# Two edits at the seam between attention and feed-forward: one load moved to GpSimd's queue, and an attention scope whose pools are laid in another order

## The chip, the cores and the metric

The kernel runs on one core of one Trainium2 chip. The metric is device microseconds (us) of one launch, less is better. A launch is timed several times and the median is given; one further execution was recorded by the hardware profiler, and the views below are read from its trace. Engines are named as the profile names them: PE (TensorE matmul), PEld (its weight loads), DVE (VectorE), ACT (ScalarE), POOL (GpSimd), SP (SyncE, which does nothing here but issue DMAs). SPq, ACTq and POOLq mark what an engine's queue does beside computing, DMA issues above all.

## The reference, cut to what matters

Four images of 64 x 64 pixels and 256 channels, in f32, pass through two layers:

```python
# layer 0: group norm, deformable convolution (8 groups x 9 bilinear samples), residual
x = x + conv(_gn(x), ...)
# layer 1, on 4096 tokens an image: additive attention, then a feed-forward part for half the tokens
t = t + attn(_ln_t(t), Wt, Wx, bh, Wa, ba)
t = t + ffn(_ln_t(t), wr, br, w1, b1, w2, b2)

def attn(inputs, ...):
    q = inputs @ Wt;  k = inputs @ Wx.T                  # 32 units each
    beta = tanh(q[:, :, None, :] + k[:, None, :, :] + bh)  # 4096 x 4096 x 32
    a = softmax(beta @ Wa[:, 0] + ba)
    return a @ inputs

def ffn(x, ...):
    weights = x @ wr + br                                # one number per token
    sel = the 2047 tokens with the largest weights
    y = (gelu(x[sel] @ w1 + b1) @ w2 + b2) * weights[sel]
    return x + (y at sel, 0 elsewhere)
```

## The kernel before, in words

**Stages.** After a stage that works out offsets and weights for all images and the sampling of image 0, a loop runs over the images n = 0 to 3. Each turn has two parts. In the first, three generators are advanced in a hand-written order of turns: `feed_forward(n - 1)`, `attention_prep(n)` and `sample_image(n + 1)`. In the second, `attention(n)` runs, with what is left of the sampling in its gaps. After the loop `feed_forward(3)` runs alone: the tail.

**Sampling** loads weights (`wb`, L692, two buffers) and rows (`xs`, L687) on SyncE, multiplies and adds them on DVE (L701, L709), and stores tokens from SyncE. Some "exact rows" are gathered again by an indirect DMA of GpSimd (L585, L590, into `xre`) and combined on DVE (L663, into `tte`).

**attention_prep(n)** loads the tokens, normalises and transposes them, and works out exponentials: `kf` for the keys stays in SBUF, those for the queries (`qe`, L838) are stored to DRAM (`qf_d`, by ScalarE's queue).

**attention(n)** takes 512 queries at a time. `queries(q)` loads their factors from `qf_d` into `qf` (L881, on SyncE) and makes `qn` of them (L884, two operations of GpSimd). Then, for each tile of 128 keys and each of three pairs of terms: `d` products on PE (L898), Ln into a tile `r` on ACT (L992), Exp (L994), `nn` products on PE (L908) and a quotient on DVE (L913); sums on POOL and DVE (L998, L1000, L1002, L1005), an Exp on ACT (L920), and the product with the values on PE (L936), whose result DVE adds up (L960). L859 is PE's last work of attention_prep.

**feed_forward(n)** chooses the tokens and scatters all rows by 32 indirect DMAs of GpSimd (L1304) into `sort_d`, the chosen ones first. Then it works on four chunks of 512 rows. `chunk(s)` loads the rows (L1336, its output named `big` in the profile) and waits for all 32 scatters before that. It normalises them on ACT (L1344), transposes them (`transpose4`, L784 and L785) into `xT`, and adds on POOL (L1350) and DVE (L1352). For each chunk, 8 products `ph` on PE with a gelu on ACT (L1364, L1365) and 4 products `py` on PE (L1370) follow; DVE combines (L1373), and an indirect DMA of GpSimd scatters the rows into the output (L1377). `chunk(s + 1)` is called within chunk s, after its second `py`.

**What sets the order.** The framework's planner fixes, when the kernel is built, the order of instructions in each engine's queue; each queue then runs in that order. DVE operations marked as pinned keep the order of the program; they are all recorded by one helper, line L259.

**Pools.** Tiles live in pools of SBUF. A scope lists its pools as (name, buffers, memory); those of SBUF are laid one after another in the listed order from the scope's base. A pool that lies over a pool of the scope before waits until that one is done. The scope of the first part, which stays as it is, is

```python
("one", 1, 0), ("two", 2, 0), ("sb", 2, 0), ("row", 2, 0), ("rp", 3, 0),
```

`one` holds `big`; w1 and w2 lie above it in `one`; `two` holds small statistics and `si`, `sb` small tiles, `row` the `xT`, `rp` the tiles `qe` and transposed tokens. In the attention scope `rp` holds the tiles `r` (six), `qp` holds `qf` and `qn`, `ep` the weights `et`, `ap` the sums of L960, `sb` small tiles, `tte` and `xre` among them. The tail's scope has the same names without `rp`.

Of the kernel before, what the change touches and what calls it, by code (L numbers as in the profile page):

```python
# [36 lines left out]
PVB = 8  # L37
# [8 lines left out]
def layers_kernel(ctx: ExitStack, tc: tile.TileContext, a, out: bass.AP):  # L46
    nc = tc.nc
# [192 lines left out]
    @contextmanager  # L240
    def scope(*pools):

        with ExitStack() as st:
            for name, bufs, psum in pools:
                kw = {"space": PSUM} if psum else {}
                setattr(S, name, st.enter_context(tc.tile_pool(name=name, bufs=bufs, **kw)))
            yield
            for name, _, _ in pools:
                delattr(S, name)
# [494 lines left out]
    def sample_any(n):  # L744

        num = nc.values_load(large[0:1, n : n + 1], min_val=0, max_val=L)
        with tc.If(num > P), scope(
            ("smp", 2, 0), ("two", 2, 0), ("sb", 2, 0), ("dn", 1, 0), ("ps_t", 1, 1), ("ps_m", 1, 1)
        ):
            cur = S.two.tile([P, 1], F32, tag="cur", name="cur")  # L750
            nc.vector.tensor_copy(cur, part)
            with tc.For_i(0, NT, 1):
                exact = []
                for _ in exact_rows(n, cur, exact):
                    pass
                put_rows(n, *exact[0])
                nc.vector.tensor_scalar(cur, cur, float(P), None, ALU.add)
# [21 lines left out]
    def transpose4(dst, src, vec=nc.vector):  # L779

        pt = S.ps_d.tile([P, CC, 512], F32, tag="d", name="ptt")
        for k in range(CC):
            for t in range(4):
                nc.tensor.transpose(pt[:, k, t * P : (t + 1) * P], src[:, t, k * P : (k + 1) * P], ident)  # L784
        vec.tensor_copy(dst, pt)  # L785
# [462 lines left out]
    def feed_forward(n, vec):  # L1248
# [81 lines left out]
        def chunk(s):  # L1330

            o = nh + s % 2 * nx
            xs = big[:, o : o + nx].rearrange("p (t c) -> p t c", t=4)
            o = nh + 2 * nx + s % 2 * nv
            vs = big[:, o : o + nv].rearrange("p (t c) -> p t c", t=4)
            get = nc.sync.dma_start(  # L1336
                out=xs, in_=sort_d[n][s * 512 : (s + 1) * 512].rearrange("(t p) c -> p t c", p=P)
            )
            for ins in put:
                tc.add_manual_dep(get.ins, ins.name, in_order, reason="rows in order")  # L1340
            si = S.two.tile([P, 4], I32, tag="si", name="si")
            vec.tensor_scalar(si, xs[:, :, C + 3], float(n * L), None, ALU.add)
            for t in range(4):
                nc.scalar.activation(  # L1344
                    vs[:, t, :], xs[:, t, :C], AF.Identity, bias=xs[:, t, C + 1 : C + 2], scale=xs[:, t, C : C + 1]
                )
            xT = S.row.tile([P, CC, 512], F32, tag="vT", name="xT")
            transpose4(xT, vs, vec)

            nc.gpsimd.tensor_tensor(vs, vs, xs[:, :, :C], ALU.add)  # L1350
            for t in range(4):
                vec.scalar_tensor_tensor(  # L1352
                    vs[:, t, :], b2, xs[:, t, C + 2 : C + 3], vs[:, t, :], ALU.mult, ALU.add
                )
            held[s] = xs, vs, si, xT

        chunk(0)
        yield
        for s in range(NSORT // 512):
            xs, vs, si, xT = held.pop(s)  # L1360
            for f in range(FF // P):
                ph = S.ps_m.tile([P, 512], F32, tag="pm", name="ph")
                for k in range(CC):
                    nc.tensor.matmul(ph, w1[:, k, rows(f)], xT[:, k, :], start=(k == 0), stop=(k == CC - 1))  # L1364
                S.tables.append(nc.scalar.activation(hT[:, f, :], ph, AF.Gelu_apprx_tanh, bias=b1[:, f, :]))  # L1365
            yield
            for t in range(4):
                py = S.ps_m.tile([P, C], F32, tag="pm", name="py")
                for f in range(FF // P):
                    nc.tensor.matmul(  # L1370
                        py, hT[:, f, rows(t)], w2[:, f, :], start=(f == 0), stop=(f == FF // P - 1)
                    )
                vec.scalar_tensor_tensor(  # L1373
                    vs[:, t, :], py, xs[:, t, C + 2 : C + 3], vs[:, t, :], ALU.mult, ALU.add
                )
                m = min(P, NSEL - s * 512 - t * P)
                nc.gpsimd.indirect_dma_start(  # L1377
                    out=out_rows, out_offset=bass.IndirectOffsetOnAxis(ap=si[:m, t : t + 1], axis=0),
                    in_=vs[:m, t, :], in_offset=None,
                )  # L1380
                if t == 1 and s + 1 < NSORT // 512:
                    chunk(s + 1)
                yield
# [23 lines left out]
    for n in range(NB):  # L1407
        with scope(("att", 1, 0), ("smp", 2, 0), ("dn", 1, 0)):
            v = S.att.tile([P, NT, C + 1], F32, name="v")
            kf = S.att.tile([P, 2, L], F32, name="kf")  # L1410

            sampling = sample_image(n + 1) if n + 1 < NB else iter(())
            S.gather = False
            with scope(
                ("one", 1, 0), ("two", 2, 0), ("sb", 2, 0), ("row", 2, 0), ("rp", 3, 0),
                ("ps_d", 2, 1), ("ps_n", 1, 1), ("ps_m", 3, 1),
            ):


                main = feed_forward(n - 1, pinned) if n else iter(())  # L1420
                prep = attention_prep(n, v, kf, pinned)
                if n:
                    turns = (
                        "mos" + "m" * 3 + "mo" * 8 + "om" + "oss" * 2 + "m" + "oss" * 7 + "m" + "oss" * 3
                        + ("m" + "ossss" * 3 + "msss" * 4) * 4
                    )
                else:
                    turns = "o" * 10 + "s" + "os" * 24
                for turn in turns:
                    next({"m": main, "o": prep, "s": sampling}[turn], None)  # L1430
                for rest in (main, prep):
                    for _ in rest:
                        pass
            S.gather = True
            with scope(
                ("two", 2, 0), ("sb", 2, 0), ("rp", 6, 0), ("qp", 2, 0),
                ("ep", 2 * PVB + 1, 0), ("ap", 1, 0), ("ps_d", 2, 1), ("ps_n", 3, 1), ("ps_m", 1, 1),
            ):
                attention(n, v, kf, [sampling])
        attention_any(n)  # L1440
        if n + 1 < NB:
            sample_any(n + 1)
# [39 lines left out]
```

## Time and profile before

| | |
|---|---|
| time, median of 3 runs | 10574.97 us (10574.79 to 10576.85) |
| the profiled execution, whole | 10547.94 us |
| its span in the profile | 10546.2 us |
| mean granted clock of TensorE | 0.916 |
| busy share of the span | PE 86%, PEld 42%, DVE 81%, ACT 70%, POOL 50% |
| moved by DMA | 766.00 MB, mean 73 GB/s |

The profiled execution is 27.0 us (0.26%) below the median of the timed runs.

How to read the lines shown below. The timeline of an engine has one line per group of like instructions that follow each other: start and duration in us, engine, line of the kernel, operation, output<-inputs by the program's names, shapes where they are given, how many (x3), and in brackets the time that the engine stood idle before it and what ended that idleness. "[4.41 <-DMA out_dram<-big,si]" is 4.41 us of idleness ended by the landing of a DMA from `big` (addressed by `si`) to the output. A line on SPq or POOLq is the issue of a DMA; its landing is later. The view of waits has: waiting line, releaser, then us in total, number of waits and the longest. Releasers are inferred from semaphore events.

### The profile page before, as it was taken

Reading aid. Unit: us, or ns where it says so; the run is one execution under the profiler, and the core shown is the slowest. Engines: PE = TensorE matmul, PEld = TensorE weight load, DVE = VectorE, ACT = ScalarE, POOL = GpSimd, SP = SyncE. Lnnn points to the kernel's source line nnn. Section 1 sums busy time; section 2 is a strip of 40 time slices with the busy share of each in tenths; the row PEclk is TensorE's granted clock in tenths of the full one; section 3 lists DMA queues with packets and bytes.
Section 4 is the critical chain, followed back from the end, with each engine's and each line's share of the span. In section 5 each row is a group of like instructions: output and inputs, shape, how many; then the busy total and the mean of one; then the engine's idle time right before and its main releaser. Section 6 shows DMA issues by size and latency. Waiting matters only on the chain. (4 is left out here: it accounts for less than half of the span.)

```text
span 10546.2 us, 115935 instructions
## 1 busy us (share of the span) xinstructions
PE 9022.3 (86%) x38460; PEld 4384.6 (42%) x38460; DVE 8536.6 (81%) x13342; ACT 7374.7 (70%) x8389; POOL 5276.0 (50%) x3059
## 2 busy tenths in 40 slices
PE   7881039999999788999999689999999699999995
PEld 4541014444444343444444344444444344444443
DVE  7776879898989778989899679899898367777772
ACT  4450018888888537888888438888888379999991
POOL 0004207676555326767655327677555155555552
PEclk8995569999999888999999789999999799999997
DMA  3336642222212252212111342122111300000002
GB/s 120 108 137 184 206 164 70 61 67 61 70 64 74 95 168 63 52 54 58 53 55 51 115 154 53 53 53 55 52 57 43 101 13 9 10 8 7 7 5 75
DMA packets 381329, 766.00 MB, mean 73 GB/s; under 512 B 49104, under 2 KB 212592, under 8 KB 380688
## 3 DMA queue, kind: packets, MB, share of 16 engines
q1 hardware_dynamic: 324432, 678.78, 19.7%
q0 software_dynamic: 30144, 45.87, 2.8%
q10 hardware_dynamic: 26112, 33.56, 0.9%
q8 instruction: 309, 5.06, 0.2%
q14 instruction: 332, 2.72, 0.1%
HBM read 580.88 MB, written 177.14 MB: 72 GB/s over the span
## 5 line engine op out<-in xcount | busy, mean ns | idle before, releaser
L913 DVE TENSOR_TENSOR r<-nn,r 128x512 f32<-128x512 f32 x6144 | 3937.1, 681 | 862.2 <-PE nn L908 805.6
L908 PE MATMUL nn<-qn,kf 32*128 32x512 f32 (+1 forms) x12288 | 4518.9, 640 | 131.9 <-DVE r L913 95.7
L998 POOL TENSOR_TENSOR r<-r 128x1024 f32<-128x1024 f32 x1024 | 2709.6, 2646 | 2635.7 <-DVE r L913 2623.6
L992 ACT ACTIVATE r<-d 128x1024 f32<-128x1024 f32 x3072 | 3114.0, 1014 | 1089.0 <-DVE r L1002 693.3
L898 PE MATMUL d<-qf,kf 32*128 32x512 f32 (+1 forms) x12288 | 3341.3, 632 | 77.2 <-DMA qf<-qf 43.0
L994 ACT ACTIVATE r<-r 128x1024 f32<-128x1024 f32 x3072 | 3124.1, 1051 | 32.7
L908 PEld LDWEIGHTS nn<-qn,kf 32*128 32x128 f32 (+1 forms) x12288 | 1399.4, 185 | 1896.4 <-DVE r L913 1443.2
L936 PE MATMUL pv<-v,et 128*128 128x257 f32 x8192 | 2107.1, 401 | 15.0 <-DVE acv L960 15.0
L936 PEld LDWEIGHTS pv<-v,et 128*128 128x128 f32 x8192 | 1509.9, 194 | 980.5 <-issue 772.8
L898 PEld LDWEIGHTS d<-qf,kf 32*128 32x128 f32 (+1 forms) x12288 | 1018.1, 186 | 1340.3 <-issue 725.1
L1000 POOL TENSOR_TENSOR r<-r 128x512 f32<-128x512 f32 x1024 | 1332.7, 1301 | 95.8 <-DVE r L913 20.6
L701 DVE TENSOR_TENSOR prd<-xs,wb 128x1024 f32<-128x1024 f32 x768 | 974.5, 1269 | 51.2 <-DMA wb<-wt 48.2
L709 DVE TENSOR_TENSOR ac<-ac,prd 128x1024 f32<-128x1024 f32 x768 | 996.2, 1297 | 8.8
L630 POOL DMA_INDIRECT ga<-tab,tii x576 | 727.1, 1262 | 208.2 <-issue 116.3
L920 ACT ACTIVATE et<-et,nshift 128x512 f32<-128x512 f32 x1024 | 723.9, 707 | 28.2 <-DVE et L1005 28.2
L1002 DVE TENSOR_TENSOR r<-r 128x512 f32<-128x512 f32 x1024 | 720.9, 704 | 4.1 <-POOL r L998 3.7
L1005 DVE TENSOR_TENSOR et<-r 128x512 f32<-128x512 f32 x1024 | 695.7, 679 | 0.4
L115 ACT ACT_TABLE_LOAD x9 | 11.5, 1283 | 797.9 <-DVE mv L259 700.0
L725 PE MATMUL pmo<-outwp,ac 128*128 128x256 f32 x512 | 136.1, 416 | 469.6 <-DVE ac L709 431.9
L480 POOL MEMSET w<- 128x1600 f32 x16 | 22.9, 1432 | 674.3 <-DVE red L456 386.4
L725 PEld LDWEIGHTS pmo<-outwp,ac 128*128 128x128 f32 x512 | 100.9, 205 | 522.1 <-DVE ac L709 305.1
L420 PE MATMUL pc<-xn,diag 128*128 128x512 f32 x576 | 262.6, 610 | 33.4 <-ACT xn L366 33.4
(344 smaller groups left out, 5278.9 us busy)
## 6 DMA issues: line engine op xcount, KB each, us to landing
wb<-wt SPq DMA_DIRECT2D x800, 512.0 KB
tab<-tb SPq DMA_DIRECT2D x128, 256.0 KB
v<-t SPq DMA_DIRECT2D x64, 512.0 KB
xs<-xp SPq DMA_DIRECT2D x32, 680.0 KB
xp<-xp SPq DMA_DIRECT2D x32, 544.0 KB
xt<-in_x_dram SPq DMA_DIRECT2D x32, 512.0 KB
xr<-in_x_dram SPq DMA_DIRECT2D x64, 256.0 KB
t<-xr SPq DMA_DIRECT2D x64, 256.0 KB
```

What stands on the lines that cost most here:

```text
L630: keep(nc.gpsimd.indirect_dma_start(out=ga[:, s, dy].rearrange("p c e -> p (c e)"), out_offset=None, in_=tab_d[n], in_offset=bass.Indirect ...
L701: keep(nc.vector.tensor_tensor(pr.rearrange("p (r w) -> p r w", w=W), src, wb.rearrange("p (r w) -> p r w", w=W), ALU.mult,))
L709: keep(nc.vector.tensor_add(ac[:, f, :], ac[:, f, :], pr))
L898: keep(nc.tensor.matmul(d[:, j, :], kf[g, blk, rows(kt)], qs[q][0][g, blk, :], start=True, stop=True))
L908: keep(nc.tensor.matmul(nn, kf[g, blk, rows(kt)], qs[q][1][g, blk, :], start=True, stop=True))
L913: keep(nc.vector.tensor_tensor(r[:, j, :], ns[j], r[:, j, :], ALU.mult))
L920: keep(nc.scalar.activation(ets[b], ets[b], AF.Exp, bias=nshift))
L936: keep(nc.tensor.matmul(pv, ets[b0 + i][:, rows(j)], v[:, k0 + i, :], start=(i == 0), stop=(i == PVB - 1)))
L992: keep(nc.scalar.activation(rs[b, p], ds.pop((b, p)), AF.Ln))
L994: keep(nc.scalar.activation(rs[b, p], rs[b, p], AF.Exp, scale=-1.0))
L998: keep(nc.gpsimd.tensor_tensor(rs[b, 1], rs[b, 1], rs[b, 2], ALU.add))
L1000: keep(nc.gpsimd.tensor_tensor(rs[b, 1][:, 0], rs[b, 1][:, 0], rs[b, 3][:, 0], ALU.add))
```

## The change

The load of the first chunk's sorted rows (`chunk(0)`, four times in the program: one per feed-forward part) is issued by GpSimd's queue; those of chunks 1 to 3 stay on SyncE's. In the attention scope the six pools of SBUF are listed in another order: `rp` and `qp` change places with `ep` and `ap`, so that `ep` follows `sb`, then `rp`, `ap` and `qp`. Buffers, sizes and the PSUM pools stay.

```diff
@@ chunk(s), in feed_forward @@
-            get = nc.sync.dma_start(
+            get = (nc.sync if s else nc.gpsimd).dma_start(
                 out=xs, in_=sort_d[n][s * 512 : (s + 1) * 512].rearrange("(t p) c -> p t c", p=P)
             )
             for ins in put:
@@ the scope around attention(n) @@
             with scope(
-                ("two", 2, 0), ("sb", 2, 0), ("rp", 6, 0), ("qp", 2, 0),
-                ("ep", 2 * PVB + 1, 0), ("ap", 1, 0), ("ps_d", 2, 1), ("ps_n", 3, 1), ("ps_m", 1, 1),
+                ("two", 2, 0), ("sb", 2, 0), ("ep", 2 * PVB + 1, 0), ("rp", 6, 0), ("ap", 1, 0), ("qp", 2, 0),
+                ("ps_d", 2, 1), ("ps_n", 3, 1), ("ps_m", 1, 1),
             ):
```

## The prediction, made before the changed kernel was run

> **What bounds the kernel now.** I read the page first: PE, DVE and ACT are busy 86%, 81% and 70% of the span, and the chain that ended last reaches back only through the tail, so it judges neither edit. Both edits sit in the stretches between one image's attention and the next, and in the tail. There I read SyncE's own waits, then the timelines engine by engine.
>
> SyncE's waits (waiting line, releaser, us in total, times, longest):
>
> ```profile
> SPq L881 <- DMA out_dram<-big,si: 33.9, 5, 11.6
> SPq L1336 <- DMA sort<-v,rif: 27.0, 2, 25.8
> ```
>
> L881, the load of the query factors, waits for the last scatters of the feed-forward; L1336, the load of sorted rows, for the scatters into `sort`. In the stretch before image 1's attention, SyncE's queue at the second wait (start, us, what), and the engines it holds up:
>
> ```profile
> 3713.26 6.79 SPq L692 DMA_DIRECT2D wb<-wt  x3
> 3750.05 0.71 SPq L1336 DMA_DIRECT2D big<-sort  x1
> 3750.78 0.00 SPq L692 DMA_DIRECT2D wb<-wt  x1
> 3750.82 0.39 SPq L1336 DMA_DIRECT2D big<-sort  x1
> ```
> ```profile
> 3755.30 1.22 DVE L701 TENSOR_TENSOR prd<-xs,wb 128x1024 f32<-128x1024 f32 x1 [19.33 <-DMA wb<-wt]
> ```
> ```profile
> 3752.36 2.07 ACT L1344 ACTIVATE big<-big 128x256 f32<-128x256 f32 x4 [18.78 <-DMA big<-sort]
> ```
>
> No `wb` load leaves for 30 us, and DVE starves for 19.33 us of them (16.52 us before image 2's attention; image 3 has no sampling beside it). Two sorted-row loads leave together: the first is `chunk(0)`, the second `chunk(1)`, 0.77 us behind it. Next, the end of the same stretch on POOL, SP, PE, ACT and DVE:
>
> ```profile
> 3964.43 2.55 POOL L1377 DMA_INDIRECT out_dram<-big,si  x1 [4.41 <-DMA out_dram<-big,si]
> 3975.50 0.99 POOL L590 DMA_INDIRECT xre<-in_x_dram,rii  x1 [8.52 <-DMA out_dram<-big,si]
> 3978.79 3.11 POOL L884 TENSOR_SCALAR qn<-qf,csel 128x512 f32<-128x512 f32 x2 [2.29 <-DMA qf<-qf]
> ```
> ```profile
> 3974.80 0.55 SPq L881 DMA_DIRECT2D qf<-qf  x1
> ```
> ```profile
> 3978.83 2.09 PE L898 MATMUL d<-qf,kf 32*128 32x512 f32 x8 [13.64 <-DMA qf<-qf]
> ```
> ```profile
> 3981.07 1.94 ACT L992 ACTIVATE r<-d 128x1024 f32<-128x1024 f32 x2 [53.99 <-PE d L898]
> ```
> ```profile
> 3982.64 0.42 DVE L663 TENSOR_TENSOR tte<-xre,outb 128x256 f32<-128x256 f32 x1 [16.90 <-DMA xre<-in_x_dram,rii]
> 3986.39 1.29 DVE L913 TENSOR_TENSOR r<-nn,r 128x512 f32<-128x512 f32 x2 [1.96 <-PE nn L908]
> ```
>
> The last scatter lands at T = 3974.8; then follow one after another the load of `qf` (4.0 us), the first `d` products (2.2), Ln (3981.07) and the first quotient (3986.39). DVE has done nothing since 3966.
>
> **Query factors.** Who waits for whom here follows from the order of the pools. Added up from the tile sizes, the feed-forward scope lies in bytes per partition from its base at: `one` 0 to 54,240 (`big` is its first 33,280), `two` to 56,864, `sb` to 73,312, `row` to 81,504, `rp` to 93,792. Attention before: `sb` 0 to 12,416, `rp` to 36,992, `qp` to 53,376, `ep` to 88,192. After: `sb` to 12,416, `ep` to 47,232, `rp` to 71,808, `ap` to 75,936, `qp` to 92,320. Before, `qf` lies over w1 and w2, whose last reader (L1364, L1370) is a matmul; still it waits for the scatters out of `big`. So waits go by whole pools. After, `qp` lies over `row` and `rp` alone: it is free when the last `ph` has read xT and the last `qe` is stored (issued 3916.3; gelu's last wait on `ph` ends at 3925). `qf` then loads at about 3930 by my estimate (3974.80 before), and the `d` products stand behind L859, which ends near 3965, at the latest.
>
> But `rp` itself still reaches into `one` (47,232 is below 54,240). The first Ln writes an `r` tile, so it now waits for T. The stall moves from L881 to L992, and what goes is the load plus two matmuls:
> - Image 1: Ln 3981.07 to about 3974.85, 6.2 us. Image 2: 6274.14 against T = 6267.96, 6.2. Image 3: 8494.82 against 8488.57, 6.2.
>
> What is late next? The first quotient comes 5.3 us after Ln in images 1 and 3 (4.9 in image 2), so 6.2 us is the gain in image 3, where no sampling stands on DVE. In images 1 and 2 DVE's queue holds `tte`, two 0.14 us copies and an L709 of 1.20 us ahead of that quotient, 1.9 us in all, and `tte` waits for `xre`, a gather that can't leave before T (`sb` lies over `one`). It left at T + 0.7 and took 7.1 us beside two `qf` loads of 512 KB. Before image 0's attention, without those, it took 5.0 us (1592.11 to 1597.10). I take 5.0: `tte` at T + 5.7, quotient at T + 7.6. That is 3982.4 for 3986.39, a gain of 4.0, and 6275.6 for 6279.09, a gain of 3.5. With 7.1 us it would be 1.9 and 1.4.
>
> `qn` (L884, 2 x 1.56 us) moves too: from T, where DVE stands idle, to POOL's queue around 3930, between scatters, where DVE samples without pause until 3966 and so sets T. POOL has gaps there (11.1 us before 3948.09). What it does to DVE is seen in two rows: beside L1350 an L701 took 3.05 us instead of 1.22; beside `qn` in attention (4095.65) an L701 took 1.43. Bounds per image 0 to 3.1 us; I take 1.5 for images 1 and 2, 0 for image 3. The Trainium skill, "SBUF — State Buffer", section "SBUF: two separate sides", speaks against this move: a DVE instruction with two SBUF inputs and a GpSimd one that reads SBUF lock each other out for the whole instruction. By that rule alone both halves would be paid in full, 3.1 us an image; the 1.43 us row says less.
>
> Image 0's load already left early (1536.5) and its pools lie free: nothing. Sum: 4.0 + 3.5 + 6.2 - 3.0 = 10.7 us gained.
>
> **First rows by GpSimd.** Removed: one 0.71 us issue per image on SyncE, and the wait ahead of it. But the wait is not gone: `chunk(1)` stays on SyncE, depends on the same 32 scatters, needs nothing else, and stood one `wb` load behind. It takes the place. At best that one `wb` slips ahead: an L701, a `mm` and an L709, 3.1 us of DVE work, in images 1 and 2. I take 0. Moved past: on POOL the load stands behind the 32nd scatter, which it waits for; behind it is L1350, which needs the load's own rows, so nobody else waits.
>
> Cost: no row shows a plain load on POOL. The nearest is the scatter of 128 rows, 0.96 us; for 512 rows 0.96 to 3.84 us against 0.71 on SyncE, so 0.25 to 3.1 us later; or it gains up to 0.7, as the two loads no longer issue one behind the other. I take 0.5, since in the tail both chunks' transposes (x16 until 10418.4) run before the first `ph` and the second load's landing (10414.98) rules. In images 1 and 2, ACT waits 18.78 us at L1344 with a `qe` behind it, so the delay passes on. Four times 0.5 is 2.0 us; ends -2.8 and +12.4. "DMA: Bandwidth & Descriptors", section "Latency and other measured facts", gives about 1 us to the first byte from GpSimd and 0.6 from SyncE; by it four loads would lose an estimated 1.6 us. No run here shows it.
>
> Total: 10.7 - 2.0 = 8.7 us less. The profiled execution took 10547.94 us (span 10546.2 plus 1.7) and would take 10539.2; the median of the runs is 27.0 us higher and I carry the difference over: 10575 - 9 = 10566.
>
> **Rivals.**
> - Forecast, 10566 (0.48): stalls move to L992 and to `chunk(1)`. Bad end: with 7.1 us for `xre` the gains are 1.9 + 1.4 + 6.2 = 9.5; both `qn` paid in full take 2 x 3.1 = 6.2, the dearest loads 12.4: 10575 - 9.5 + 6.2 + 12.4 = 10584. Good end: gains 13.7, a `wb` slip of 2 x 3.1, `qn` free, loads -2.8: 10575 - 13.7 - 6.2 - 2.8 = 10552.
> - The whole gain is eaten, 10575 (0.07): the terms of the bad end, in part.
> - SyncE is really freed, 10535 (0.17): `chunk(1)` is queued behind more `wb` loads, and `qe` goes ahead of L1344 on ACT. Then up to 19.3 + 16.5 = 36 us of DVE idleness go; I count 31 of them, since a first `wb` still has to land, on top of the forecast's 9: 10575 - 40. Against: `chunk(1)` left 0.77 us behind `chunk(0)`.
> - `r` doesn't wait for T, 10540 (0.10): Ln starts when `py` is done, near 3966, 9 us sooner in three images, 27 in all. Against: whole-pool waits at L881, and 47,232 < 54,240.
> - Slower, 10602 (0.18): the early `qf` load is queued on SyncE ahead of `wb` loads and waits there for the last `ph` as L1336 does now. It decides once the wait outlasts the two `wb` buffers, some 5 us of L701 and L709; at the present stalls' size it costs 19.3 + 16.5 = 36 us; less the gain of 10.7 and with 2.0 for the loads that is 27 more, 10602. For it: this queue already holds two such waits. Against: `ph` is done before DVE's last ten L701 (from 3925 on).
>
> **How the numbers follow.** About 0.2%, 21 us, is what a measurement of this kernel can tell from no change. Faster by more: 0.17 + 0.10 = 0.27; slower by more: 0.18; within: 0.48 + 0.07 = 0.55. The forecast's own range is 10552 to 10584; to leave no more than 2 in 10 out it reaches down to 10540 and up to the slower rival's 10602, which leaves out only the freed queue (0.17).
>
> **What would show it.** Right: L881 issues near 3930 with no wait on `out_dram`; L992's idle time ends on that scatter, 0.1 us after T; `d` long done; L701 still starves 13 to 19 us before `chunk(1)` leaves SyncE; the `sort` load on POOL takes 1 to 4 us. Wrong: a `wb` load between 3720 and 3750; Ln before the last scatter lands; SyncE waiting at L881 with `wb` behind it.

## The result, and the profile after

The changed kernel took 10577.8 us, median of 12 runs, and the kernel before 10575.74 us beside it: a ratio of 1.0004, interval 0.9995 to 1.0013. In a second comparison (the last experiment below) the ratio was 1.0011, from 1.0001 to 1.0020. Together that is some 0.07%, 8 us, slower and no change by the bound of the prediction; the forecast gain of 9 us lies outside both intervals. The profiled execution's span was 10568.6 us. Spans of single executions differ by more than what is looked for here, since stages that the change doesn't touch vary by several us, so the traces are compared by distances within a seam (the stretch between one image's feed-forward part and the next attention).

First, the sorted rows ahead of image 1's attention. The views are the timelines of SP, POOL, DVE and ACT of the changed kernel, with the columns as before.

```profile
3741.17 0.37 SPq L1336 DMA_DIRECT2D big<-sort  x1
```
```profile
3738.51 0.96 POOL L1304 DMA_INDIRECT sort<-v,rif  x1 [0.30 <-DMA sort<-v,rif]
3741.68 0.81 POOL L1336 DMA_DIRECT2D big<-sort  x1 [2.20 <-DMA sort<-v,rif]
```
```profile
3746.60 1.23 DVE L701 TENSOR_TENSOR prd<-xs,wb 128x1024 f32<-128x1024 f32 x1 [28.22 <-DMA wb<-wt]
```
```profile
3744.84 0.60 ACT L1344 ACTIVATE big<-big 128x256 f32<-128x256 f32 x1 [32.15 <-DMA big<-sort]
3749.14 1.58 ACT L1344 ACTIVATE big<-big 128x256 f32<-128x256 f32 x3 [3.71 <-DMA big<-sort]
3750.64 1.00 ACT L839 ACTIVATE qe<-pf 128x1024 f32<-128x1024 f32 x1
```

One row on SyncE is `chunk(1)`, and it stands where `chunk(0)` stood: DVE still starves for `wb` until it has left, 28.22 us here and 25.6 in image 2. That is no growth: the second trace of the kernel before (the null run below) has 24.7 and 27.1 us there, and in the first one part of the same idleness stood at other waits. The load on POOL lands later than the one on SyncE, although it was issued only 0.51 us behind it: in this trace 7.4 us after its issue, at 3749.1. The planner has put one operation of chunk 1 ahead of chunk 0's: ACT normalises a row group of chunk 1 at 3744.84, then waits 3.71 us more for chunk 0, and the `qe` behind it starts 12.1 us after the last scatter into `sort` (3738.51). Before it was 8.4 us (3745.96 to 3754.34).

Then the seam into image 1's attention, on SP, POOL, ACT and DVE.

```profile
3915.32 1.20 SPq L881 DMA_DIRECT2D qf<-qf  x2
...
3965.08 0.81 SPq L964 DMA_DIRECT2D tr<-t  x2
```
```profile
3954.38 2.92 POOL L1377 DMA_INDIRECT out_dram<-big,si  x1 [2.65 <-DVE big L259]
3957.35 3.39 POOL L884 TENSOR_SCALAR qn<-qf,csel 128x512 f32<-128x512 f32 x2
3965.84 1.07 POOL L590 DMA_INDIRECT xre<-in_x_dram,rii  x1 [5.10 <-DMA out_dram<-big,si]
```
```profile
3972.63 1.94 ACT L992 ACTIVATE r<-d 128x1024 f32<-128x1024 f32 x2 [55.48 <-DMA xr<-in_x_dram]
```
```profile
3971.74 0.43 DVE L663 TENSOR_TENSOR tte<-xre,outb 128x256 f32<-128x256 f32 x1 [12.73 <-DMA xre<-in_x_dram,rii]
3972.08 0.14 DVE L259 TENSOR_TENSOR lo<-lo 1x1 f32<-1x1 f32 x1
3972.25 0.14 DVE L259 CAST wide<-lo 1x1 int32<-1x1 f32 x1
...
3977.64 1.89 DVE L913 TENSOR_TENSOR r<-nn,r 128x512 f32<-128x512 f32 x3 [4.11 <-PE nn L908]
```

The query factors are loaded 50 us ahead of T, as the edit says. T, the landing of the last scatter, is about 3965.05 here: L964 leaves then, having waited for it. But Ln does not start at T; it starts 7.6 us later. The bracket names a load of `xr`, which no part of Ln reads; what ends 0.24 us ahead of Ln is the copy into `wide` (3972.25 + 0.14), the last reader of `lo`, a tile of the old pool `two` over which the new `rp` lies. In image 2 it is the same 0.24 us. `wide` stands on DVE behind `tte`, which waits for `xre`, which waits for T. The first quotient comes 23.3 us after the issue of the last scatter; before it was 22.0. In image 2 it is 22.9 for 21.9.

In image 3, which has no `tte`, the seam looks as forecast at its end, but not ahead of it: POOL, SP and ACT of the changed kernel.

```profile
8490.94 0.96 POOL L1377 DMA_INDIRECT out_dram<-big,si  x1 [17.46 <-DVE big L259]
8494.10 0.96 POOL L1377 DMA_INDIRECT out_dram<-big,si  x1 [2.20 <-DVE big L259]
8499.67 0.96 POOL L1377 DMA_INDIRECT out_dram<-big,si  x1 [4.61 <-DMA out_dram<-big,si]
8503.01 2.55 POOL L1377 DMA_INDIRECT out_dram<-big,si  x1 [2.37 <-DMA out_dram<-big,si]
```
```profile
8492.32 1.21 SPq L881 DMA_DIRECT2D qf<-qf  x2
```
```profile
8514.18 1.94 ACT L992 ACTIVATE r<-d 128x1024 f32<-128x1024 f32 x2 [24.27 <-DMA out_dram<-big,si]
```

Ln waits for the last scatter alone, and the first quotient comes 16.5 us after its issue instead of 23.0. But the third scatter now waits 4.61 us, for an earlier one's landing, 7 us after 1 MB of query factors was asked for. In the kernel before:

```profile
8467.26 0.96 POOL L1377 DMA_INDIRECT out_dram<-big,si  x1 [17.50 <-DVE big L259]
8470.43 0.96 POOL L1377 DMA_INDIRECT out_dram<-big,si  x1 [2.21 <-DVE big L259]
8473.67 0.96 POOL L1377 DMA_INDIRECT out_dram<-big,si  x1 [2.29 <-DVE big L259]
8477.16 2.55 POOL L1377 DMA_INDIRECT out_dram<-big,si  x1 [2.52 <-DVE lsm L259]
```

From the first to the last of these four there are 12.1 us after the change and 9.9 before it.

### The profile page after: what moved, and what is told of

The parts are those of the page before. It is cut to its first block, busy times and chain, and to the rows that moved or that the text cites. A ratio compares the mean times of both kernels' runs of the same rounds, so it can differ in the third digit from the quotient of the medians.

```text
span 10568.6 us, 115934 instructions
## 1 busy us (share of the span) xinstructions
PE 9008.8 (85%) x38460; PEld 4376.6 (41%) x38460; DVE 8547.5 (81%) x13342; ACT 7377.3 (70%) x8389; POOL 5282.9 (50%) x3063
## 3 DMA queue, kind: packets, MB, share of 16 engines
q1 hardware_dynamic: 322320, 676.65, 19.6%
## 5 line engine op out<-in xcount | busy, mean ns | idle before, releaser
L908 PE MATMUL nn<-qn,kf 32*128 32x512 f32 (+1 forms) x12288 | 4523.4, 641 | 133.6 <-DVE r L913 97.2
L998 POOL TENSOR_TENSOR r<-r 128x1024 f32<-128x1024 f32 x1024 | 2710.5, 2647 | 2662.2 <-DVE r L913 2622.7
L992 ACT ACTIVATE r<-d 128x1024 f32<-128x1024 f32 x3072 | 3117.5, 1016 | 1097.3 <-DVE r L1002 707.5
L701 DVE TENSOR_TENSOR prd<-xs,wb 128x1024 f32<-128x1024 f32 x768 | 982.6, 1279 | 70.8 <-DMA wb<-wt 68.1
L1005 DVE TENSOR_TENSOR et<-r 128x512 f32<-128x512 f32 x1024 | 697.2, 681 | 0.4
L480 POOL MEMSET w<- 128x1600 f32 x16 | 22.9, 1432 | 672.7 <-PE ptw L497 386.1
```

Source lines behind the costliest of these rows:

```text
L701: keep(nc.vector.tensor_tensor(pr.rearrange("p (r w) -> p r w", w=W), src, wb.rearrange("p (r w) -> p r w", w=W), ALU.mult,))
L908: keep(nc.tensor.matmul(nn, kf[g, blk, rows(kt)], qs[q][1][g, blk, :], start=True, stop=True))
L992: keep(nc.scalar.activation(rs[b, p], ds.pop((b, p)), AF.Ln))
L998: keep(nc.gpsimd.tensor_tensor(rs[b, 1], rs[b, 1], rs[b, 2], ALU.add))
```

## Experiments

Theory A, from the traces: the order of pools moves the wait onto `wide` in images 1 and 2, gains some 5 us in image 3, and gives it back because the early loads collide with the last scatters; the load by GpSimd lands a few us late and part of that is paid. The rivals were that one of the two edits does nothing and the traces differ by chance, that the queue of GpSimd carries the late Ln, and that the lower clock of TensorE takes the gain back. Every experiment was timed in five rounds against the kernel before, on the same chip as the others of its batch.

**Each edit alone.** First the new order, all loads on SyncE (the upper half of the change's diff left out).

> Only the new order of pools; all sorted rows are loaded by SyncE as before. Theory A (the wait moved on to DVE): the first tile r now also lies over the old pool `two`, so the first Ln waits for the copy into `wide`, which stands on DVE behind `tte`, which waits for the gather of `xre`, which waits for the last scatter. From the issue of the last scatter to the first quotient: 23.2, 22.9 and 16.5 us in images 1, 2 and 3 (before 22.0, 21.9, 23.0), and from the last of the 32 scatters to the next `qe` 8.4 us as before. In all 1.3 + 1.0 - 6.5 = 4 us less than before, 0.04%. Theory B (the load on GpSimd's queue carries the late Ln, since both DMAs share POOL's queue): distances of 18, 18 and 16.5 us, 14 us less than before.

Measured: 10559.69 us, ratio 1.0006 (0.9997 to 1.0015). From the last scatter to the first quotient 23.7, 22.8 and 16.5 us; from the last scatter into `sort` to the next `qe` 8.7 and 8.9. So the late Ln belongs to the order of pools, not to the queue. The 4 us were not found in the time: the interval allows at most 3 of gain.

Then the load alone, in the old order of pools, twice.

> Only the load of the first sorted rows by GpSimd's queue; pools in the old order. Theory A (a slow landing): the load lands 7.4 us after its issue instead of 2.3, ACT's normalising stands ahead of a `qe`, so the `qe` comes 12 us after the last of the 32 scatters instead of 8.4 in images 1 and 2; in image 3 and the tail the first gelu comes 1.6 and 0.8 us later. In all some 9 us more than before, 0.09%. From the last scatter into the output to the first quotient 22, 22 and 23 us as before. Theory B (the queue makes no difference; what the two traces differ by between these points is spread from one execution to the next): `qe` after 8 to 9 us, the time within 3 us of before.

> The same as e2_get_only, once more: its time read 0.14% slower, while its trace shows no stage that is longer by more than 1 us (last scatter into `sort` to last scatter into the output 215.0, 217.3, 157.5 and 126.4 us, in the two traces of before 218.5 and 216.6, 214.6 and 214.1, 157.5 and 155.8, 126.6 and 125.4). Theory A (the load on GpSimd's queue is 2 to 4 us slower at landing, but little waits for it): a ratio of 1.0000 to 1.0005. Rival: it costs 9 us or more, 1.0009 or above once more.

Measured: 10559.74 us, 1.0014 (1.0005 to 1.0023), and 10576.45 us, 1.0010 (1.0001 to 1.0020). It does cost, about 0.12%, 13 us: more than the 9 of theory A in the first expectation, and in the second the rival was right. In images 1 and 2 `qe` came 9.5 and 11.9 us after the last scatter into `sort` in the first trace, 12.4 and 11.6 in the second; the first quotients came after 22.2, 22.5 and 23.1 us and after 22.0, 22.7 and 22.9, as in the old order.

From the last scatter into `sort` to the last one into the output, summed over images 1 to 3, the traces give: both edits left out 590.5 and 586.5 us (the kernel before and the null run below), the load alone 589.7 and 602.7, both edits 602.0 and 610.4. That is 8 us for the load, with up to 13 us between two traces of one kernel; the tail adds under 1 us. That the load costs something is shown by the two times; its size, 8 to 13 us, is an estimate.

**`r` over the old place, `qf` and `qn` over the new one.**

```diff
-                ("two", 2, 0), ("sb", 2, 0), ("rp", 6, 0), ("qp", 2, 0),
-                ("ep", 2 * PVB + 1, 0), ("ap", 1, 0), ("ps_d", 2, 1), ("ps_n", 3, 1), ("ps_m", 1, 1),
+                ("two", 2, 0), ("sb", 2, 0), ("rp", 6, 0), ("ep", 2 * PVB + 1, 0), ("ap", 1, 0), ("qp", 2, 0),
+                ("ps_d", 2, 1), ("ps_n", 3, 1), ("ps_m", 1, 1),
```

> All loads by SyncE; pools in the order sb, rp, ep, ap, qp: `r` lies over the old `one` alone (as before the change), `qf` and `qn` over `row` and `rp` alone (as after it). Theory A: the first Ln starts 0.1 us after the last scatter has landed in all three images, as `wide` no longer holds it up; the first quotient then stands behind `tte` in images 1 and 2, 18 us after the issue of the last scatter, and 16.5 in image 3; 4 + 4 + 6.5 = 14 us less than before, 0.14%. Rival: Ln waits for something that the order of pools doesn't move (the landing of `xr`, as the releaser reads), and the distances stay at 23, 23 and 16.5: 4 us less than before.

Here `r` lies over `one` and not over `two`, so that `wide` can't hold Ln. SP, ACT and DVE of this kernel at image 1:

```profile
3967.94 0.81 SPq L964 DMA_DIRECT2D tr<-t  x2
```
```profile
3967.97 1.94 ACT L992 ACTIVATE r<-d 128x1024 f32<-128x1024 f32 x2 [47.61 <-DMA out_dram<-big,si]
```
```profile
3974.45 0.42 DVE L663 TENSOR_TENSOR tte<-xre,outb 128x256 f32<-128x256 f32 x1 [15.59 <-DMA xre<-in_x_dram,rii]
3974.80 0.14 DVE L259 TENSOR_TENSOR lo<-lo 1x1 f32<-1x1 f32 x1
3974.97 0.14 DVE L259 CAST wide<-lo 1x1 int32<-1x1 f32 x1
3976.18 1.87 DVE L913 TENSOR_TENSOR r<-nn,r 128x512 f32<-128x512 f32 x3
```

Ln starts as the last scatter lands, 7 us ahead of `wide`, and the first quotients come after 18.6, 19.0 and 16.5 us: the wait on `wide` is shown, and so is the place of `tte`, which now holds up the quotient instead. Followed further, the 16th block's first sum on POOL (L998) starts 133.6, 134.2 and 119.0 us after that scatter, and in four traces with the old order 136.5 to 139.2, 135.6 to 140.6 and 123.7 to 125.8: 4, 4 and 5 to 6 us were kept. Yet the time was 10555.53 us, 1.0003 (0.9994 to 1.0013), not 14 us less. Part of what is gained after T had been lost before it: there were 30.6 and 30.8 us between the 12th and the 13th of the 16 scatters into the output in images 1 and 2 (27.2 to 28.9 and 27.5 to 28.7 in the old order), and 11.9 us from the first to the last of the last four in image 3 (9.9). From the 12th to the last scatter that is some 7 us of the 14; where the rest went is not shown.

**Half of the early bytes.** The kernel of the last experiment, with the second block of factors held back until the first Ln; the same kernel was timed twice.

```diff
-            nc.sync.dma_start(out=qf, in_=qf_d[n][:, :, q * QB : (q + 1) * QB])
+            ld = nc.sync.dma_start(out=qf, in_=qf_d[n][:, :, q * QB : (q + 1) * QB]); q and tc.add_manual_dep(ld.ins, lns[0], in_order, reason="late")
```

`lns[0]` is the first Ln; the two lines that fill `lns` are left out here.

> As e3_r_low, but the second block of query factors (512 KB, needed some 240 us later) is loaded only after the first Ln; the first block stays early. Theory A (the early loads collide with the feed-forward's last chunk): with 1 MB of early loads the third scatter of image 3's last chunk waited 4.4 us for a landing instead of 2.3, and the last scatter came 159.1 to 159.4 us after the last scatter into `sort` instead of 155.8 to 157.5; between the 12th and the 13th scatter of images 1 and 2 there were 30.2 to 30.6 and 30.8 to 32.1 us instead of 27.3 to 29.0 and 27.4 to 28.7. Half the bytes: at least half of that goes, 156 to 158.5, under 29.5 and under 30 us. 2 + 1 + 1 = 4 us less than e3_r_low. Rival: the delay comes from the order on SyncE's queue (the loads stand ahead of token stores), not from the bytes; the one load left costs as much as two.

> The same as e9_low_late, once more (`r` low, first query factors early, the second block after the first Ln, all sorted rows by SyncE): its time read 0.9994 with an interval from 0.9985 to 1.0003. Theory A (seams: 4 us earlier in images 1 and 2, 5 to 6 in image 3, nothing given back ahead of the last scatter): 0.9985 to 0.9993, and between the 12th and 13th scatter 27 to 29 us in images 1 and 2. Rival (what the seam gains is lost later): 1.0000 or more.

Measured: 10554.78 us, 0.9994 (0.9985 to 1.0003), and 10544.7 us, 0.9992 (0.9983 to 1.0001). The first trace has 28.6 and 28.3 us between the 12th and 13th scatter in images 1 and 2, and 9.9 for the last four in image 3: the delay is gone. The second has 30.2, 30.2 and 10.4: in image 1 nothing of it is gone, in image 2 about half, in image 3 most. So that was a miss in part (27 to 29 had been expected), and so was the way from the last scatter into `sort` to the last one into the output in image 3, which took 160.6 and 156.4 us for an expected 156 to 158.5. First quotients came after 19.5, 18.9 and 16.5 us and after 19.2, 19.0 and 16.5. The 16th block's first sum came after 137.5, 135.5 and 117.3 us and after 134.2, 133.3 and 118.9; the 137.5 is no gain at all. The collision is seen in all traces with both blocks early, and half of the bytes lessen it; that it goes with the bytes rather than with the place on the queue is likely, not settled. This version reads some 7 us below the kernel before in both comparisons; neither interval alone excludes no change.

**SyncE really freed.** Loads of chunks 0 and 1 on ScalarE's queue in the three images, pools in the old order.

```diff
-            get = nc.sync.dma_start(
+            get = (nc.scalar if s < 2 and n < NB - 1 else nc.sync).dma_start(
```

> Pools in the old order; the loads of chunk 0 and of chunk 1 are issued by ScalarE's queue in the three images (the tail keeps SyncE). Theory A: in the change SyncE was not freed because chunk 1 stayed on it with the same wait. Here no load on SyncE waits for the 32 scatters, so `wb` loads go on; DVE runs on until the reduction `least`, which waits for `kf` on ACT behind the normalising: some 10 us of the 16 to 28 us of idleness at `wb` go in images 1 and 2, 16 to 20 us less than before, 0.17%. Rival: the idleness only moves from `wb` to `least` and comes back in full: within 4 us of before.

Measured: 10554.49 us, 1.0005 (0.9996 to 1.0014); the rival was right. DVE of this kernel in image 1:

```profile
3734.01 0.75 DVE L259 TENSOR_SCALAR mm<-pq,bqk 128x512 f32<-128x512 f32 x1 [5.93 <-remote]
...
3745.29 1.22 DVE L259 COPY vT<-ptt 128x1024 f32<-128x1024 f32 x1 [8.13 <-remote]
...
3754.78 1.22 DVE L259 TENSOR_REDUCE least<-pk 128x1 f32<-128x1024 f32 x1 [5.88 <-ACT kf L832]
```

No wait of over 2.2 us at `wb` is left, but 5.93 + 8.13 + 5.88 = 19.9 us stand at `mm`, `vT` and `least` in its place, as 19.33 had stood at `wb`; in image 2 all of it, 26.64 us, stands at `least`. ACT is held by the same 32 scatters, and with it the `qe` and `kf` that come next; the view names `kf` for the wait at `least`, and only "remote" for the other two. A kernel in which ACT too is free of that wait was not tried.

**The clock.** As `r` low, with the second `d` product of the first block repeated.

```diff
-            for j, (blk, g) in enumerate(parts(pair)):
+            for j, (blk, g) in list(enumerate(parts(pair))) * (1 + (0, 9, 9, 21)[n] * ((b, pair) == (0, 1))):
```

> As e3_r_low, and the second `d` product of each attention's first block is repeated, 9 times in images 1 and 2 and 21 times in image 3, with the same operands and the same result, so that TensorE has something to do while Ln waits. Theory A (the clock takes back half of the gain): the granted clock fell to 0.50 while TensorE waited, and 8 us of work at that clock came after the first Ln instead of ahead of it. With the repeats the clock is 1.00 when the last scatter lands; the first quotient in image 3 comes 14 to 15 us after that scatter's issue (e3_r_low 16.5), and the end of attention 3 some 1801 us after it (e3_r_low 1804.6, before 1808.1). All together 3 x 3 = 9 us less than e3_r_low. Rival: the clock at the start doesn't matter further on, since DVE sets the pace; the end of attention 3 stays at 1804 to 1805.

Measured: 10574.83 us, 1.0007 (0.9998 to 1.0016). The repeats were too many: they ended after the landing in all three images, and Ln waited for them (21.1, 18.3 and 18.3 us after the issue of the last scatter, against 10.4, 10.7 and 11.2 in e3_r_low). So neither the whole time nor the forecast end of attention 3 (1801 us; it was 1809.6) can be read here. What can be read is image 3 from Ln on, where the clock was 1.00 in this trace and 0.50 at Ln in all others. From Ln to the first L998 there were 6.6 us here, 7.9 to 8.1 in the six traces whose clock came back 4.7 to 5.8 us after Ln (the kernel before among them), and 9.0 in the seven where it came back after 9.4 to 10.8 us (e3_r_low and the changed kernel among them). From that first L998 the 16th came 98.7 us later and the last 1781.7; in e3_r_low 98.8 and 1781.3. So the half clock at the start costs 1.3 to 2.4 us in image 3 and nothing further on, and the old order pays it too (9.0 in the null run): the clock is not where the gain went. In images 1 and 2 the repeats left the clock at 0.50, and nothing is tested there.

**A sixth buffer less**, so that `r` could lie clear of `one` and `two`, and its control.

```diff
-                ("two", 2, 0), ("sb", 2, 0), ("rp", 6, 0), ("qp", 2, 0),
-                ("ep", 2 * PVB + 1, 0), ("ap", 1, 0), ("ps_d", 2, 1), ("ps_n", 3, 1), ("ps_m", 1, 1),
+                ("two", 2, 0), ("sb", 2, 0), ("ep", 2 * PVB + 4, 0), ("ap", 1, 0), ("rp", 5, 0), ("qp", 2, 0),
+                ("ps_d", 2, 1), ("ps_n", 3, 1), ("ps_m", 1, 1),
```

> All loads by SyncE; pools in the order sb, ep, ap, rp, qp, `rp` with five buffers instead of six and `ep` with three more, so that `r`, `qf` and `qn` lie over the old `sb`, `row` and `rp` alone and over neither `one` nor `two`. Theory A: Ln waits for no scatter into the output. It starts within 2 us of the first `d`; in image 3 the first quotient comes some 6 to 7 us after the issue of the last scatter (before 23.0) and TensorE's clock stays at 1.00, so that the gain of 16 us lasts to the end of that attention (1792 us after the scatter, before 1808). In images 1 and 2 the quotient still stands behind `tte`, at 18 us, with several Ln and Exp done ahead: 4 us each. In all some 24 us less than before (0.23%), less what the sixth buffer was worth. Rival: early work at the seam is given back within the attention, and the end of attention 3 moves by 5 us at most.

> The kernel before with five buffers for `r` instead of six; nothing else. It sizes what e7_r_high5 pays for its fifth buffer: if Ln runs ahead into the sixth buffer, each attention takes longer than 1902, 1901 and 1785 us from the first to the last quotient in images 1, 2 and 3. Theory A: no more than 3 us each, since ACT is idle a tenth of the time. Rival: ACT is held up at every block, 10 us or more in each.

Measured: 11448.95 us, 1.0834 (1.0819 to 1.0849), and for the control 11421.82 us, 1.0815 (1.0798 to 1.0832). Both theories on the fifth buffer were far off: the order of the attention is written out for six tiles `r`, and with five Ln waits for the freeing sum at nearly every block (there are 1024). ACT's waits in the control:

```profile
ACT r L992 <- DVE r L1002: 1109.3, 976, 4.3
ACT r L992 <- DVE et L1005: 376.8, 829, 1.9
```

Before it was 693.3 us in 726 waits, and no wait of L992 for L1005. Together that is 793 us more of waiting, beside 850 us more of time. In images 1 and 2 Ln did start early (5.7 and 2.8 us after the issue of the last scatter), the first quotient stayed behind `tte` (19.6 and 18.5), and by the fourth block nothing was left: its first L998 came after 45.4 and 44.3 us, 45.1 and 45.3 in the control. In image 3 the pools behind `sb` lie some 4 KB lower, since no sampling has a tile there, and `r` still touched `one` and Ln waited for T (11.2 us). So the gain of 16 us expected there was not tested.

**Controls.** The kernel before as its own rival, and the changed kernel again.

> The kernel before, unchanged, timed as if it were another one. It shows how far two equal kernels lie apart in such a comparison, and gives a second trace of the old seams. Theory A (the seams tell more than the time): a ratio within 0.999 to 1.001; from the last scatter into the output to the end of image 3's attention 1808 us, as in the two other traces with the old order (1808.1, 1808.4). Rival: the ratio lies at 1.0005 or more, as it did for all four kernels of the first batch, so that whatever is timed second reads some 5 us longer.

> The changed kernel once more, beside the two others on the same chip. Theory A, added up from the seams: 1 us later at the first quotient of images 1 and 2, 2 to 3.5 us later at their last scatter for the early loads, 5 us earlier at the end of attention 3 less 2 us for the collision there, and 1 to 2 us for the first rows: 1.0002 to 1.0007. Rival (the seams give nothing away, the kernel gains the 9 us of the forecast): 0.9992.

Measured: 0.9999 (0.9990 to 1.0008), so the comparison has no bias that shows, and 1.0011 (1.0001 to 1.0020), above what theory A added up to, though its range lies within the interval. The null run's end of attention 3 came 1812.1 us after the last scatter, not 1808, so that distance varies by 4 us; distances to fixed blocks vary less, and those are used above. The second trace of the changed kernel repeats the first: `qe` after 9.9 and 12.1 us, 30.4 and 31.8 us between the 12th and 13th scatter of images 1 and 2, first quotients after 23.5, 23.3 and 16.6 us.

## Why the prediction was right, and where it was not

Its verdict held: no change by its bound. Its main reason held too, that both stalls move and do not go. But the 9 us of gain did not come, and the sum came out as some 8 us of loss; that the verdict is right all the same owes something to luck, since errors of either sign stayed below the bound of 21 us. By its own steps:

- **`chunk(1)` takes the wait of `chunk(0)`**: right. DVE starved 28.2 and 25.6 us for `wb`; the 13 to 19 us that the text gave as a sign came from one trace, and the null run has 24.7 and 27.1.
- **The load by GpSimd, 0.5 us each, 2.0 in all**: mis-sized. From the last scatter into `sort` to ACT's first work on most of chunk 0 there were 6.4 to 7.5 us in images 1 to 3 with SyncE (nine traces) and 7.9 to 10.9 with GpSimd (four traces). About 8 us by the traces and 13 by the time are paid, near the far end of 12.4 that the text kept. The choice of 0.5 rested on the issue alone; the landing was the cost, and the planner's order, which let a piece of chunk 1 go ahead, was not thought of.
- **Ln at T in images 1 and 2**: this is the step that failed in its mechanism. The layout in the text shows it: `rp` at 47,232 to 71,808 covers the end of `one` and all of `two` (54,240 to 56,864), where `lsm`, `lo` and their kin lie. The text stopped at the first pool. Ln stood behind `wide`, hence behind `tte`, and a forecast gain of 4.0 + 3.5 us became a loss of about 1 us each at the first quotient and none that shows later.
- **Image 3, 6.2 us**: 6.5 at the first quotient, about 5 from the 16th block to the end of that attention.
- **The early load at no cost**: this term was missing. With both blocks early, the 13th scatter comes 2.3 and 3.7 us later behind the 12th in images 1 and 2, and the last of image 3 comes 1.8 us later behind the 13th, all ahead of T. In image 1 of the changed kernel the last four scatters then went faster (13.3 and 13.6 us for 14.1 to 16.4), so that from the 12th to the last its two traces lost 0.3, 4.2 and 2.2 us, 6.7 in all. The slower rival had the place, but its mechanism, a wait on SyncE's queue, wasn't there: L881 left at 3915.32 with `wb` loads 0.6 us ahead.
- **`qn` beside sampling, 3.0 us**: not so. It stands on POOL behind the last scatter, where it meets the end of one L701 in image 1. That one took 1.59 us in the first trace of the changed kernel and 1.23 in the second, with much the same overlap, and the first `qn` 1.83 and 1.88 us instead of 1.56. The row of 1.43 us on which the text leaned was one side alone: there L701 had started 0.31 us ahead, and it was `qn` that took 3.06 us instead of 1.56. The lock of the shared port that the prediction cited is not settled by such rows.
- **Rivals**: SyncE was not freed, and e4_two_act shows that freeing it gains nothing as long as ACT is held too. `r` did wait for T, and longer.

The sum as measured: 8 us for the loads, 6.7 for the collision, 5 gained in image 3, some 10 us more; the two times say 8, with about 7 on either side. From the forecast's 8.7 of gain one comes there by 7.5 for Ln in images 1 and 2, 6.0 for the loads, 6.7 for the collision and 1.2 for image 3, less 3.0 for `qn`.

## What to carry to other kernels

When a pool is moved, list every old pool that the new place covers, and for each the last instruction that touches it and what that one is queued behind; the latest of them is the new wait, and it may be a 1x1 copy behind a gather. A load that is made earlier runs beside other transfers, so look at who waits for a landing there. Before a stall at one queue is removed, look for a second engine held by the same event: here ACT waited for the same 32 scatters, and the idleness only changed its label.

## What the runs showed of the hardware

TensorE's granted clock falls to 0.50 while TensorE idles at a seam and comes back some time after it works again. In image 3 of the kernel before it fell 2.7 us after the last product (8477.35) and came back 7.9 us after the first new one (8492.65). The time to come back was not the same everywhere: 3.4 and 3.2 us in images 1 and 2 of the changed kernel (products from 3973.71 and 6284.7 on), 12.7 us in image 1 of the kernel before. PE and its clock in four stretches of the kernel before, at image 3 (stretch, us, busy us and instructions, clock, DMA share, GB/s), then in the changed kernel at image 1, then in e6_low_warm at image 2:

```profile
8476.00:8480.00 4.00, 0.71 (x4) 1.00 0.00 0
8480.00:8492.00 12.00, 0.00 (x0) 0.50 0.22 59
8492.00:8500.00 8.00, 6.20 (x21) 0.50 0.39 127
8500.00:8508.00 8.00, 7.94 (x36) 0.97 0.00 0
```
```profile
3961.00:3973.00 12.00, 0.00 (x0) 0.50 0.48 127
3973.00:3977.00 4.00, 3.29 (x12) 0.50 0.23 66
3977.00:3981.00 4.00, 3.96 (x20) 0.99 0.00 0
```
```profile
6281.00:6298.00 17.00, 17.00 (x44) 0.50 0.36 91
6300.00:6308.00 8.00, 8.00 (x24) 0.50 0.00 1
6308.00:6312.00 4.00, 3.94 (x19) 0.93 0.49 131
```

In the third, 17 us of unbroken products of 32 rows left the clock at 0.50, and it rose only some 9 us into the attention's own mix of products. In image 3 the same repeats began at 1.00 and kept it there for 19 us. The Trainium skill, "TensorE: Matmul & The Clock Gate", section "Part 1: The HAM clock gate (the "warmup" mystery)", gives about 4 us of sustained products for the rise and about 3.4 us of idleness for the fall. The fall came 0.9 to 4.2 us after the last product in image 3 of the thirteen traces in which it fell there. The rise agrees in the changed kernel's images 1 and 2 and took much longer elsewhere, in the third view with TensorE busy all the time, so being busy is not all that the clock goes by. What it does go by was not tried.
